# Moving ScalarE's copies out of PSUM behind other work, in a kernel whose order is planned step by step

## The chip, the cores and the metric

One core of one Trainium2 chip runs the whole kernel. Its engines take their instructions in the order in which the program issued them: TensorE (PE; its weight loads are listed as PEld), VectorE (DVE), ScalarE (ACT), GpSimd (POOL) and SyncE (SP, which here only starts transfers). The metric is the device time of one execution in microseconds. Before the change it is 3862.21 us, the median of 13 runs (3836.64 to 3873.43).

## The reference, cut to what matters

Sixteen graphs (B) of 1024 nodes (N) with 64 channels (C); the adjacency matrix is dense in float32, with about 1 in 64 entries nonzero. Four graph layers follow one another, each with a residual and a layernorm:

```python
def reference(x, adj, nodemask, ...):
    # 0: plain graph convolution
    x = _layernorm(x + einsum('bnm,bmo->bno', adj, x @ w0) + b0)
    # 1: thin the neighbours of nodes with more than 10 of them (every skip-th by rank),
    #    then, per node and channel, 0.25/0.5/0.75 quantiles of the neighbours' values
    adj_d = _dilate_adj(adj, nodemask)
    agg = _weighted_nanquantile_agg(x, adj_d > 0)      # sorts, weights 0.25, 0.5, 0.25
    y = relu((x + agg) @ W1 + b1) @ W2 + b2
    x = _layernorm(x + y * nodemask)
    # 2: three layers of messages over the adjacency, 128 wide
    h = x @ W_embed
    for i in range(3):
        h = relu(adj @ (h @ Wl[i] + bl[i]))
    x = _layernorm(x + (h @ W_proj + b_proj) * nodemask)
    # 3: aggregate and compare
    t = adj @ x
    return _layernorm(x + where(t > 0.5, t / t, t * 0.0))
```

## The kernel before, in words

**Tiles.** A graph has T = 8 blocks of 128 nodes (P = 128). A row of 1024 is handled in NH = 2 halves of 512 columns (HALF), which is one PSUM bank of float32; TH = 4 blocks make a half. The tile `adjT` (in the profile `adjB`) holds the transposed adjacency of one graph, 4 MB.

**Strands.** Each graph is worked on by several generators, called strands here:

- `words_of` (line 559): `transposed` (L483) loads the adjacency by blocks of rows, transposes each on PE (L496, two halves of four 128x128 transposes, each half in a bank of the PSUM ring `tp`) and lets ACT copy each half to SBUF (L498, tile `at`; its DMA to DRAM as `adjd` is L590, on ACT's queue). One block later its function `words` compares the block with zero on DVE (L583, L585, tile `nb`), feeds layer 0 (`Layer0.feed`, 8 matmuls at L521 into the single bank `ax`), and packs each row's neighbour bits into words with 8 matmuls (L594, a bank of `tp`), which ACT copies out as `hi` and `lo` (L597, L598). After the fourth and the eighth block ACT copies the bank of layer 0 out (L526). `Layer0.end` (L529) transposes x (L535, ring `tp`), copies it (L537), and finishes the first layer (L542 and a layernorm).
- `front` and `listing` (L613, L647): rank the nodes by their number of neighbours, permute them with one-hot matmuls (L717 on DVE, L722 and L723 on PE), find the neighbours' indices from the words (DVE, L768 to L793), and write a table of node values to DRAM.
- `gathered`, `masked`, `quantiles`, `summed`, for each of five groups of blocks: POOL gathers neighbours' rows from the table (L918); ACT adds a mask to each gathered column of rows (L973); DVE sorts with a network of minima and maxima (L1023); ACT multiplies the sorted rows by weights (L1059) and PE adds them up in the bank `pa` (L1052).
- `back` (L1250): all that follows the quantiles. `to_nodes` (L1083) brings the sums back to the order of the nodes: ACT makes a one-hot matrix for each block from `iota` in two instructions (L1102, L1103, tile `ones_at`, two buffers) and PE multiplies by it (L1107). Then come the two dense layers of layer 1, `to_channels` (L416), three times messages (L1324, copied at L1327) and aggregation (L1335, copied with a ReLU at L1338), the projection, and layer 3 (`aggregate`, L426; L431, copied at L434). Its banks come from the ring `mm`.

The PSUM rings: `mm` 2 banks, `tp` 2, `wd` 2, `ax` 1, and `pa` with part of one. A bank is taken again when the copy out of it is done.

**The order.** Nothing is scheduled by the framework. At the end of the kernel (L1361 to L1431) all strands stand in one queue, sorted by due time. The strand with the smallest due time is run to its next `yield`; what it issues meanwhile goes to the engines' queues in this order, and the yielded number, times the strand's stretch, is added to its due time:

```python
        add(ready - LISTS - WORDS, words_of(state[b]), WORDS / WORDS_STEPS)
        add(start((b + 1) * G) + AFTER, back(state[b]), BACK / BACK_STEPS)
        ...
            dt = next(steps, None)
            if dt is not None:
                heapq.heappush(queue, (t + dt * stretch, order, steps, stretch))
```

So a `yield` is not a wait of the chip: it says how far behind this point, in planned microseconds, the strand's next instruction is put among those of the other strands. A planned graph takes 192.06 us (the sum of LENGTHS, L52). The stretch of `words_of` is 152.6/82, that of `back` 178/181. At a time, the words of one graph, the lists and sorts of others and the back of an earlier one are interleaved.

Of the kernel before, what the change touches and what calls it, by code (L numbers as in the profile page):

```python
# [53 lines left out]
WORDS_STEPS, LISTS_STEPS, BACK_STEPS = 82.0, 74.0, 181.0  # L54
# [152 lines left out]
def kernel(  # L207
# [191 lines left out]
    def psum_tp():  # L399
        return psum("tp", 2)  # L400
# [4 lines left out]
    def psum_ax():  # L405
        return psum("ax", 1)
# [9 lines left out]
    def to_channels(dst, src):  # L416

        for h in range(NH):
# [3 lines left out]
            yield 1.5  # L422
            nc.scalar.copy(dst[:, h * HALF:(h + 1) * HALF], pt[:C, :])
            yield 1.0

    def aggregate(dst, adjT, src, bank):  # L426

        for h in range(NH):
# [5 lines left out]
            nc.scalar.copy(dst[:, h * HALF:(h + 1) * HALF], pa[:C, :])  # L434
            yield 0.7
# [47 lines left out]
    def transposed(b, block, then):  # L483
# [4 lines left out]
        late = None  # L488
        for t in range(T):
            a = ahead[t]  # L490
            at = block(t)
            for h in range(NH):
                pt = psum_tp()
                for i in range(TH):
                    j = h * TH + i
                    nc.tensor.transpose(pt[:, i * P:(i + 1) * P], a[:, j * P:(j + 1) * P], ident)  # L496
                yield 1.2
                nc.scalar.copy(at[:, h * TH:(h + 1) * TH, :],  # L498
                               pt.rearrange("p (i n) -> p i n", n=P))
                yield 0.8  # L500
            if t + AHEAD < T:
                ahead.append(load_row(b, t + AHEAD))
            if late:
                yield from late
            late = then(t, a, at)
        yield 1.0
        yield from late

    class Layer0:
# [6 lines left out]
        def feed(self, t, at):  # L516
            if t % TH == 0:
                self.bank = psum_ax()
# [5 lines left out]
            if t % TH == TH - 1:  # L524
                h = t // TH
                nc.scalar.copy(self.ax[:C, h * HALF:(h + 1) * HALF], self.bank[:C, :])  # L526
                yield 0.7

        def end(self, y):  # L529
            for h in range(NH):  # L530
                pt = psum_tp()
                for i in range(TH):
# [3 lines left out]
                yield 1.0  # L536
                nc.scalar.copy(self.ax[C:, h * HALF:(h + 1) * HALF], pt[C:, :])  # L537
                yield 0.7
# [7 lines left out]
            yield 1.0  # L546
# [12 lines left out]
    def words_of(st):  # L559
# [21 lines left out]
        def words(t, a, at):  # L581
# [4 lines left out]
            if b:  # L586
# [3 lines left out]
                nc.scalar.dma_start(adjd[:, t], at)  # L590
            pw = psum_tp()
# [5 lines left out]
            nc.scalar.copy(hi[:, t, :W], pw[:, :W])  # L597
            nc.scalar.copy(lo[:, t, :], pw[:, W:2 * W + 2])  # L598
            yield 0.6
# [434 lines left out]
    def summed(st, g):  # L1034
# [33 lines left out]
        yield 1.5  # L1068
# [14 lines left out]
    def to_nodes(dst, st):  # L1083
# [12 lines left out]
        for s in range(T):  # L1096
            ones_at = tmp.tile([P, N], BF16, tag="ones_at", name="ones_at", bufs=2)
# [13 lines left out]
        for h, bank in enumerate(banks):  # L1111
# [3 lines left out]
            yield 1.2  # L1115
            nc.scalar.copy(dst[:, h * HALF:(h + 1) * HALF], bank[:C, :])
        yield 1.0
# [131 lines left out]

    def back(st):  # L1250
# [225 lines left out]
```

## Time and profile before

| | us |
|---|---|
| median of 13 runs | 3862.21 |
| the profiled execution | 3866.06 |
| its span, first to last instruction | 3864.3 |
| DVE busy | 2801.8 (73%) |
| PE busy (matmuls) | 2707.7 (70%) |
| POOL busy | 2173.2 (56%) |
| ACT busy | 1902.9 (49%) |
| L1335, aggregation of messages, PE, 1536 records | 818.0, mean 0.653 |
| L973, masks, ACT, 2272 instructions | 597.3, mean 0.339 |
| L498, block of the adjacency out of PSUM, ACT, 240 | 138.0, mean 0.576 |

How it is read: a row of the profile names the line, the engine, the operation, what it writes and reads, how often, the busy time and the mean of one in nanoseconds, and behind the last bar the idle time of the engine just before such instructions with what ended it. "A <- B: 218.2, 31, 20.5" in a list of waits means that A stood idle 218.2 us in all until B ended, 31 times, 20.5 at the longest. "issue" is time in which an engine waited for nothing the profile shows; "remote" is a wait that ended with a signal for which the profile has no instruction ending at that time. The granted clock is the share of TensorE's full clock that was granted: 0.80 on average. The mean TensorE busy time contains time at the lower clock.

### The profile page before, as it was taken

How to read it: one execution, taken by the hardware profiler on the slowest of the kernel's cores; microseconds unless marked ns; L12 is line 12 of the kernel's file. 1: busy time of each engine (PE TensorE's matmuls, PEld its weight loads, DVE VectorE, ACT ScalarE, POOL GpSimd, SP SyncE). 2: the span in 40 equal slices, each digit the busy share in tenths (PEclk: the TensorE clock that was granted, in tenths of full speed). 3: DMA queues.
4: the chain of work that ended last, by engine and by line, in shares of the span. 5: the costliest groups of instructions: out<-in, count | busy, mean ns of one | idle time of the engine just before them, and what ended most of it. 6: DMA issues, size and time to landing. Idle time of an engine off the chain costs nothing.

```text
span 3864.3 us, 49100 instructions
## 1 busy us (share of the span) xinstructions
PE 2707.7 (70%) x13765; PEld 1625.2 (42%) x13766; DVE 2801.8 (73%) x8020; ACT 1902.9 (49%) x6153; POOL 2173.2 (56%) x2078
## 2 busy tenths in 40 slices
PE   6234596867768686686768768677776868675587
PEld 5233353534445353443435444444443535343343
DVE  6287787968687796878769686787867879687561
ACT  2234555545465644545455454636445554545451
POOL 0566655565565655566555665665556556657600
PEclk8656797878878887888878788788887978867788
DMA  3222233232232332223232232323313233212110
GB/s 110 57 78 59 52 83 86 82 93 63 56 98 77 93 82 79 74 61 102 67 92 81 73 85 62 97 73 91 82 36 103 78 87 83 79 23 69 23 50 4
DMA packets 169080, 282.73 MB, mean 73 GB/s; under 512 B 99486, under 2 KB 102113, under 8 KB 166881
## 3 DMA queue, kind: packets, MB, share of 16 engines
q1 hardware_dynamic: 67584, 142.01, 11.1%
q0 software_dynamic: 66048, 69.88, 10.9%
q10 hardware_dynamic: 35168, 67.62, 4.6%
q8 instruction: 114, 1.87, 0.2%
q14 instruction: 166, 1.35, 0.1%
HBM read 204.33 MB, written 71.44 MB: 71 GB/s over the span
## 4 chain that ended last, share of the span: by engine, by line
PE 41%; DVE 19%; another core or an unknown queue 16%; ACT 14%; issue 7%; DMA 1%; POOL 1%; ACTq 0%; DVEq 0%; POOLq 0%
PE mm L1335 15%; PE mm L431 5%; DVE s L1023 5%; DVE g L1023 4%; PE ax L521 4%; ACT g L973 4%; PE mm L1107 3%; PE pa L1052 3%; ACT ones_at L1102 3%; ACT ones_at L1103 2%; PE tp L496 2%; PE mm L1324 2%; ACT g L1059 2%; DVE top L789 1%
## 5 line engine op out<-in xcount | busy, mean ns | idle before, releaser
L918 POOL DMA_INDIRECT g<-table,idx x1952 | 2053.5, 1052 | 1415.5 <-issue 416.9
L1335 PE MATMUL mm<-adjB,msg 128*128 128x512 f32 x1536 | 818.0, 653 | 95.4 <-issue 76.7
L1023 DVE TENSOR_TENSOR s<-g 128x384 f32<-128x384 f32 (+8 forms) x1200 | 577.1, 495 | 281.7 <-ACT g L973 226.6
L973 ACT ACTIVATE g<-g,bias 128x64 f32<-128x64 f32 (+9 forms) x2272 | 597.3, 339 | 82.4 <-DVE bias L969 47.2
L1023 DVE TENSOR_TENSOR g<-s 128x256 f32<-128x256 f32 (+10 forms) x1040 | 508.6, 501 | 27.9 <-remote 14.1
L1052 PE MATMUL pa<-g,ident 128*128 128x128 f32 (+1 forms) x1600 | 342.2, 338 | 208.8 <-ACT g L1059 140.1
L1052 PEld LDWEIGHTS pa<-g,ident 128*128 128x128 f32 x1600 | 284.9, 232 | 358.9 <-ACT g L1059 183.1
L1335 PEld LDWEIGHTS mm<-adjB,msg 128*128 128x128 f32 x1536 | 285.7, 206 | 333.0 <-issue 306.9
L1059 ACT ACTIVATE g<-g,w 128x64 f32<-128x64 f32 x1552 | 392.9, 337 | 13.8 <-DVE w L1030 13.2
L1107 PE MATMUL mm<-ones_at,pieces 128*64 128x512 bf16 x768 | 254.7, 480 | 202.2 <-ACT ones_at L1103 161.3
L521 PE MATMUL ax<-at,xt 128*64 128x128 f32 x1920 | 281.7, 304 | 29.4 <-issue 28.1
L431 PE MATMUL mm<-adjB,x 128*64 128x512 f32 x512 | 274.1, 670 | 11.7 <-DVE x L468 8.9
L521 PEld LDWEIGHTS ax<-at,xt 128*64 128x64 f32 x1920 | 243.3, 154 | 87.6 <-issue 83.0
L496 PE MATMUL tp<-ident,arow 128*128 128x128 f32 x1024 | 176.9, 303 | 86.6 <-ACT lo L598 60.7
L1107 PEld LDWEIGHTS <-pieces 128*64 128x64 bf16 x768 | 97.0, 131 | 315.2 <-issue 272.3
L1023 DVE TENSOR_TENSOR g<-g,s 128x256 f32<-128x256 f32 (+5 forms) x512 | 208.8, 415 | 24.8 <-remote 16.8
L1023 DVE TENSOR_TENSOR g<-g 128x256 f32<-128x256 f32 (+7 forms) x432 | 214.2, 506 | 3.8 <-DVE g L1023 1.5
L1102 ACT ACTIVATE ones_at<-iota,minus 128x1024 bf16<-128x1024 f16 x123 | 140.2, 1140 | 155.1 <-remote 101.1
L496 PEld LDWEIGHTS tp<-ident,arow 128*128 128x128 f32 x1024 | 137.1, 158 | 151.0 <-issue 80.6
L722 PE MATMUL wd<-hi,perm 128*128 128x71 f16 x960 | 107.3, 224 | 132.4 <-DVE perm L717 97.2
L597 ACT CAST hi<-tp 128x64 f16<-128x64 f32 x128 | 26.6, 208 | 352.0 <-remote 204.0
L1338 ACT ACTIVATE hlT<-mm 128x512 f32<-128x512 f32 x96 | 57.2, 596 | 267.6 <-PE mm L1335 190.5
(223 smaller groups left out, 4262.8 us busy)
## 6 DMA issues: line engine op xcount, KB each, us to landing
arow<-in_adj_dram SPq DMA_DIRECT2D x128, 512.0 KB
adjd<-at ACTq DMA_DIRECT2D x120, 512.0 KB
adjB<-adjd SPq DMA_DIRECT2D x15, 4096.0 KB
g<-table,idx POOLq DMA_INDIRECT x1952
table<-xc ACTq DMA_DIRECT2D x16, 264.0 KB
xt<-in_x_dram SPq DMA_DIRECT2D x16, 256.0 KB
out_dram<-y SPq DMA_DIRECT2D x16, 256.0 KB
stage<-table,packed POOLq DMA_INDIRECT x112
```

The costliest lines, as they stand in the source:

```text
L431: nc.tensor.matmul(pa[:C, :], src[:, m, :], adjT[:, h * TH:(h + 1) * TH, m, :], start=(m == 0), stop=(m == T - 1))
L496: nc.tensor.transpose(pt[:, i * P:(i + 1) * P], a[:, j * P:(j + 1) * P], ident)
L521: nc.tensor.matmul(self.bank[:C, cols], self.xt[:, m + 1, :], at[:, m, :], start=(m == 0), stop=(m == T - 1))
L722: nc.tensor.matmul(pw[:, :hn], ws, hi[:, t, :], start=False, stop=False)
L918: g = nc.gpsimd.indirect_dma_start(out=dst, out_offset=None, in_=st["table"], in_offset=bass.IndirectOffsetOnAxis(ap=index, axis=0))
L973: nc.scalar.activation(v, v, AF.Identity, bias=bias[:m, i, k:k + 1])
L1023: vector.tensor_tensor(box(bufs[mode >> 1 & 1], d, run, sd, count, tile), box(bufs[mode >> 3], a, run, sa, count, tile), box(bufs[mode >> ...
L1052: nc.tensor.matmul(pa[:, :(e - k) * nt * C], ident, rows_.rearrange("p (k c) -> p k c", c=R)[:, :, :C], start=(j == 0), stop=(j == len(run ...
L1059: nc.scalar.activation(slots(g, bufs[0], lo + r, lo + r + 1)[:, i, 0, :C], slots(g, bufs[at[r]], lo + r, lo + r + 1)[:, i, 0, :C], AF.Iden ...
L1102: nc.scalar.activation(ones_at, iota, AF.Abs, bias=st["minus"][:, s:s + 1])
L1107: nc.tensor.matmul(bank[:C, :], pieces[:, i, s, :], ones_at[:, h * HALF:(h + 1) * HALF], start=(s == 0 and i == 0), stop=False)
L1335: nc.tensor.matmul(pg, msg[:, m, :], adjT[:, h * TH:(h + 1) * TH, m, :], start=(m == 0), stop=(m == T - 1))
```

## The change

No instruction is added and none is removed; the steps are put in another order, by moving `yield`s and the calls between them.

- Adjacency (`transposed`): both halves of a block are transposed first. The copy of the first half is issued after the feed of the block before (at a `yield None` in `words`), the copy of the second half after that block's words matmuls.
- Words: `hi` and `lo` are copied not at once, but as a function `write` that is kept and called after the first half of the next block's transposes.
- Layer 0: the copy of the first half's bank goes just ahead of the fifth block's feed; that of the second half, and those of x, behind all transposes of `end`.
- Back: in `to_channels`, `to_nodes` and the dense layers (new function `hidden`) both halves are multiplied first, then both copied. In the message layers the copies of a half fall behind matmuls of the other half; the last half of a layer's ReLU (`late`) falls behind the first half of the next layer's messages.
- Some waits of DVE on PE's results (`residual`, the layernorm of layer 0, layer 3) get more steps ahead of them.
- `ones_at` has three buffers in place of two.
- WORDS_STEPS and BACK_STEPS, by which the stretches are formed, are 83 and 203.

```diff
-WORDS_STEPS, LISTS_STEPS, BACK_STEPS = 82.0, 74.0, 181.0
+WORDS_STEPS, LISTS_STEPS, BACK_STEPS = 83.0, 74.0, 203.0
     def to_channels(dst, src):
+        banks = []
         for h in range(NH):
             pt = psum_mm()
             for i in range(TH):
                 nc.tensor.transpose(pt[:C, i * P:(i + 1) * P], src[:, h * TH + i, :], ident)
-            yield 1.5
+            banks.append(pt)
+            yield 1.0
+        yield 2.5
+        for h, pt in enumerate(banks):
             nc.scalar.copy(dst[:, h * HALF:(h + 1) * HALF], pt[:C, :])
-            yield 1.0
+            yield 0.8
     def aggregate(dst, adjT, src, bank):
...
                 yield 1.3
-            nc.scalar.copy(dst[:, h * HALF:(h + 1) * HALF], pa[:C, :])
-            yield 0.7
+                if h and m == TH - 1:
+                    nc.scalar.copy(dst[:, :HALF], banks[0][:C, :])
+            banks.append(pa)
+        yield 3.0
+        nc.scalar.copy(dst[:, HALF:], banks[1][:C, :])
+        yield 0.7
     def transposed(b, block, then):
...
-        late = None
+        late, written = None, []
         for t in range(T):
+            banks = []
...
             for h in range(NH):
-                pt = psum_tp()
+                banks.append(psum_tp())
...
-                yield 1.2
-                nc.scalar.copy(at[:, h * TH:(h + 1) * TH, :],
-                               pt.rearrange("p (i n) -> p i n", n=P))
-                yield 0.8
+                yield 0.9
+                if h == 0 and written:
+                    written.pop()()
+                    yield 0.6
             if t + AHEAD < T:
                 ahead.append(load_row(b, t + AHEAD))
-            if late:
-                yield from late
+            def moved(h, at=at, banks=banks):
+                nc.scalar.copy(at[:, h * TH:(h + 1) * TH, :],
+                               banks[h].rearrange("p (i n) -> p i n", n=P))
+            first = True
+            for dt in late or [2.0]:
+                if callable(dt):
+                    written.append(dt)
+                elif dt is None:
+                    moved(0)
+                    first = False
+                    yield 0.7
+                else:
+                    yield dt
+            if first:
+                moved(0)
+                yield 0.7
+            moved(1)
+            yield 0.7
             late = then(t, a, at)
...
         def feed(self, t, at):
             if t % TH == 0:
+                if t:
+                    self.copied(t // TH - 1)
+                    yield 0.5
                 self.bank = psum_ax()
...
         def end(self, y):
...
-                yield 1.0
+                yield 0.7
+            yield 2.0
+            self.copied(NH - 1)
+            yield 0.6
+            for h, pt in enumerate(banks):
                 nc.scalar.copy(self.ax[C:, h * HALF:(h + 1) * HALF], pt[C:, :])
-                yield 0.7
+                yield 0.6
...
         def words(t, a, at):
...
                 nc.scalar.dma_start(adjd[:, t], at)
+            yield None
             pw = psum_tp()
...
-            nc.scalar.copy(hi[:, t, :W], pw[:, :W])
-            nc.scalar.copy(lo[:, t, :], pw[:, W:2 * W + 2])
-            yield 0.6
+            def write():
+                nc.scalar.copy(hi[:, t, :W], pw[:, :W])
+                nc.scalar.copy(lo[:, t, :], pw[:, W:2 * W + 2])
+            yield write
...
-            ones_at = tmp.tile([P, N], BF16, tag="ones_at", name="ones_at", bufs=2)
+            ones_at = tmp.tile([P, N], BF16, tag="ones_at", name="ones_at", bufs=3)
...
+    def hidden(w_sb, src, hT, copy):
+        banks = [psum_mm() for _ in range(NH)]
+        for h, ph in enumerate(banks):
+            nc.tensor.matmul(ph, w_sb, src[:, h * HALF:(h + 1) * HALF], start=True, stop=True)
+            yield 1.3
+        yield 2.0
+        for h, ph in enumerate(banks):
+            copy(hT[:, h * HALF:(h + 1) * HALF], ph)
+            yield 0.7
     def residual(src, w_sb, first, base, y):
...
-            yield 1.0
+            yield 3.5
             u = wide_u("u")
...
         for l in range(NL):
+            def give(h):
+                nc.scalar.copy(msg[:, h * TH:(h + 1) * TH, :],
+                               parts.pop(("msg", h)).rearrange("p (i k) -> p i k", k=H))
             for h in range(NH):
+                if h:
+                    if late:
+                        late()
+                        yield 0.7
                 pg = psum_mm()
...
+                parts["msg", h] = pg
+            give(0)
+            yield 1.0
+            new = act.tile([H, N], F32, tag="hT", name="hlT")
             for h in range(NH):
                 pg = psum_mm()
                 for m in range(T):
+                    if h == 0 and m == TH:
+                        give(1)
+                        yield 1.0
                     nc.tensor.matmul(pg, msg[:, m, :], adjT[:, h * TH:(h + 1) * TH, m, :],
                                      start=(m == 0), stop=(m == T - 1))
                     yield 1.3
-                nc.scalar.activation(hT[:, cols], pg, AF.Relu)
-                yield 0.7
+                    if h and m == TH - 1:
+                        nc.scalar.activation(new[:, :HALF], parts.pop("first"), AF.Relu)
+                parts["second" if h else "first"] = pg
+            def late(new=new):
+                nc.scalar.activation(new[:, HALF:], parts.pop("second"), AF.Relu)
...
-        yield 2.0
+        yield 4.0
         u = wide_u("u3")
```

## The prediction

> **What bounds the kernel now.** I read the page first, for busy shares and the chain that ended last:
>
> ```profile
> span 3864.3 us, 49100 instructions
> PE 2707.7 (70%) x13765; PEld 1625.2 (42%) x13766; DVE 2801.8 (73%) x8020; ACT 1902.9 (49%) x6153; POOL 2173.2 (56%) x2078
> PE 41%; DVE 19%; another core or an unknown queue 16%; ACT 14%; issue 7%; DMA 1%; POOL 1%; ACTq 0%; DVEq 0%; POOLq 0%
> ```
>
> No engine is full, and the chain passes from one engine to the next: the bound is waiting in fixed orders. Next came the table by stretches (columns: length, then PE, weight loads, DVE, ACT, POOL busy, granted clock, DMA share, GB/s). The first row is the steady part, where one graph takes about 228 us (the same weight-summing step recurs at 1414.7, 1643.0 and 1870.6 us in the chain); the other two lie 19 us apart inside one graph.
>
> ```profile
> 400.00:3400.00 3000.00, 2207.43 (x11360) 1309.08 (x11361) 2287.65 (x6491) 1578.04 (x5072) 1795.19 (x1705) 0.82 0.29 79
> 1434.00:1453.00 19.00, 14.68 (x85) 9.16 (x83) 18.67 (x44) 7.98 (x28) 14.09 (x13) 1.00 0.22 51
> 1453.00:1472.00 19.00, 6.45 (x16) 3.84 (x17) 4.17 (x14) 4.22 (x17) 11.04 (x11) 0.60 0.14 25
> ```
>
> DVE is busy 2288 of 3000 us, so 712 us are idle, about 54 per graph; and there are moments, like the last row, when PE, DVE and ACT all stand. Whom they wait for, over the same 3000 us (total, times, longest):
>
> ```profile
> DVE s L1023 <- ACT g L973: 218.2, 31, 20.5
> DVE u L1275 <- PE mm L1269: 47.9, 14, 11.2
> DVE perm L717 <- remote: 41.5, 9, 8.3
> DVE perm L717 <- PE mm L1107: 25.2, 6, 6.8
> DVE u L1350 <- PE mm L1347: 24.0, 11, 3.0
> PE mm L1107 <- ACT ones_at L1103: 138.5, 47, 11.5
> PE ax L542 <- ACT ax L537: 17.1, 4, 7.3
> PE mm L1335 <- ACT msg L1327: 14.7, 6, 13.2
> ```
>
> The largest wait of DVE is for the masks (L973) that ACT puts on gathered rows. Why is ACT late, at 49%? The groups by line say where it sits idle (after the second bar):
>
> ```profile
> L1102 ACT ACTIVATE ones_at<-iota,minus 128x1024 bf16<-128x1024 f16 x123 | 140.2, 1140 | 155.1 <-remote 101.1 <-PE wd L723 21.4 <-PE mm L1107 20.1
> L1338 ACT ACTIVATE hlT<-mm 128x512 f32<-128x512 f32 x96 | 57.2, 596 | 267.6 <-PE mm L1335 190.5 <-remote 58.8 <-issue 15.7
> L1327 ACT COPY msg<-mm 128x512 f32<-128x512 f32 x96 | 55.9, 582 | 204.6 <-remote 150.4 <-issue 26.5 <-PE mm L1324 26.4
> L597 ACT CAST hi<-tp 128x64 f16<-128x64 f32 x128 | 26.6, 208 | 352.0 <-remote 204.0 <-PE tp L594 123.4 <-PE pa L1052 9.4
> L537 ACT COPY ax<-tp 64x512 f32<-64x512 f32 x32 | 18.4, 581 | 153.5 <-remote 135.7 <-issue 13.0 <-PE tp L535 4.7
> ```
>
> These four copies and ones_at alone hold 1133 of ACT's 1961 us of idle time (3864.3 − 1902.9). The timeline of the standstill shows what that does:
>
> ```profile
> 1457.13 0.21 ACT L597 CAST hi<-tp 128x64 f16<-128x64 f32 x1 [14.01 <-remote]
> 1458.00 1.74 PE L1052 MATMUL pa<-g,ident 128*128 128x128 f32 x6 [9.31 <-ACT g L1059]
> 1470.01 0.60 ACT L1338 ACTIVATE hlT<-mm 128x512 f32<-128x512 f32 x1 [10.64 <-remote]
> 1471.13 0.80 PE L1052 MATMUL pa<-g,ident 128*128 128x128 f32 x2 [7.56 <-ACT g L1059]
> 1476.85 0.42 DVE L1023 TENSOR_TENSOR s<-g 128x256 f32<-128x256 f32 x1 [19.58 <-ACT g L973]
> ```
>
> ACT stands 14.0 and 10.6 us before two copies out of PSUM; behind them in its queue are the weightings (L1059) for which PE stands, and the masks for which DVE stands 19.6 us. "Remote" means that nothing the profile shows ended then: PE's signal came later than the modelled end of its matmul. I don't know why. What matters is that ACT meets it at the head of its queue.
>
> **The change, part by part.** The profiled execution took 3866.06 us (span 3864.3 and 1.8 around it), 3.85 above the median of 3862.21; I sum against 3866. The change adds no instruction and no byte: the same copies of 0.57 to 0.67 us (0.21 for hi and lo) are issued later in the planned order, so every cost is a wait.
>
> *Adjacency and words.* A block's steps run at 152.6/82 = 1.86 us of planned time before, 152.6/83 = 1.84 after. Transposes to copy: 1.2 steps (2.2 us) before; after, the first copy comes behind 0.9 + 0.6 + 0.9 + 0.3 + 2.4 = 5.1 steps (9.4 us). Words matmul to hi: 0.7 steps (1.3 us) before; 0.7 + 0.7 + 0.9 = 2.3 (4.2 us) after. What ACT loses there now (352 us at L597, 100 at L498) mostly goes.
>
> *Layer 0* (L526, L537), *back* (L1338, L1327, L434, L423, L1116): each copy falls behind 2 to 3.5 steps or behind four further matmuls of the same line. The back has more steps, but its step shrinks from 178/181 = 0.98 to 178/203 = 0.88 us, so its planned length hardly changes and its matmuls are issued a tenth denser.
>
> *Gain at the masks.* Between nothing and the 218 us of that wait. In the standstill shown, ACT lost 24.6 us at two moved copies for DVE's 19.6, so the nearest row says all; but some of what ACT is late with waits for DVE itself (the bias of the masks), and PE's late signal stays in the world. I take 60%: 130 us.
>
> *Gain from the third one-hot buffer.* With two, ACT must wait for the matmuls of two one-hots ago, PE for ACT, and DVE's permutations (L717) for PE: 41.5 + 25.2 and 14.6 more behind another matmul of PE, 81 us. ACT needs 1.14 + 1.06 us for each one-hot whatever the buffers, so between nothing and 81; I take half, 40.
>
> *Gain at u* (L1275, L1350): these waits of DVE, 47.9 + 24.0, get 3.5 and 4.0 steps in place of 1.0 and 2.0. Half: 36. In the last 214 us, the last back alone, DVE's long waits for PE are the work itself; I count nothing there.
>
> *Price: PSUM is held longer.* All rings keep their sizes (mm 2, tp 2, ax 1). So the tight side changes over: before, a bank was emptied 4 to 5.5 steps ahead of its next use; now PE's words matmul stands 0.7 steps (1.3 us) behind the copy that frees its bank, the next transposes 0.7, the second transposes 0.6, and the fifth block's feed 0.5 behind the copy of layer 0. PE takes work in order, so a late ACT now stops everything behind: feeds, L1335, the sums pa. Some 25 such links a graph in the words and 10 in the back make 490 in 14 graphs. Nearest rows: PE's waits at links that are already so short, 14.7 us over 96 message copies (0.15 each) and 17.1 over 32 copies of ax (0.53 each): 75 to 260 us of PE. Below nothing is possible only if the copies come earlier, which none does; zero is possible if ACT runs ahead. PE makes 41% of the chain: 0 to 107 us of the time. I take 0.3 a link: 147 × 0.41 = 60.
>
> The granted clock bears on that price: 1.00 while PE is busy, 0.60 in the standstill, and a pair of L1335 takes 1.02 us at 1447.7 and 1.92 at 1461.7. [...]
>
> *Queues moved past.* SP's row loads are issued between the same transposes and wait for them as before; ACT's adjacency writes wait for copies made a block earlier; the gathers on POOL follow DVE, whose order changes little. DVE's comparison of a block (L583) now stands 3.1 steps behind its last copy instead of 8: 5.7 us, ten times the copy. If ACT is later than that, DVE's sorts queue behind it.
>
> **Sum.** −130 − 40 − 36 + 60 = −146: 3866 − 146 = 3720 us.
>
> **The rivals.** *The tight links decide (slower, 0.22).* PE waits for ACT at 490 places. For it: PE is in the chain more than ACT, and already waits 138.5 us for ones_at. Against it: copies with short links now cost PE little, because ACT, with 1422 idle us in 3000, is mostly ahead. If only a third of my gains comes (69 us) and links cost 0.7 us, 343 × 0.41 = 141: 3866 − 69 + 141 = 3938. It decides from 0.34 us a link on (69/0.41/490).
>
> *Nothing is gained where it counts (0.10).* ACT's idle time is a symptom of PE's late signals; the copy waits as long in its new place, or DVE waits for the next thing, PE's sums. Then gain and price are both small: 3866 within 0.3%, 3854 to 3878. For it: 16% of the chain is time that the profile gives to no engine, and an order of copies does not touch its cause. Against it: three engines stand while the needed work lies behind one copy.
>
> *All of it goes (0.08).* −200 − 60 − 50 + 20: 3576. Then DVE would be busy 2288 of 2710 us, 84%, against 76 now; nothing forbids it, but each removed wait uncovers another.
>
> **How the numbers follow.** My forecast has 0.60, and by itself 3620 to 3845. The measurement can tell about 0.3%. Faster by more: 0.59 + 0.08 + 0.03 of the second rival = 0.70; within: 0.07 of the second rival and 0.01 of the forecast, 0.08; slower: 0.22. For 8 in 10 the range takes part of the fastest case and the nearer part of the slower one: 3580 to 3905.
>
> **What would show it.** Right: ACT's idle time at hi, hlT, msg and ax falls from 978 us to less than half; DVE's wait for the masks falls from 227 to about 90, and 19 us standstills become rare; PE shows new waits for the copies at, hi/lo and ax at transposes and words, in all 75 to 260 us. Wrong: DVE's wait for the masks stays though ACT's idle moved; or PE's waits at tp and ax exceed 300 us; or the clock falls below 0.80.

## The result: 2.0% slower, and the profile after

The changed kernel took 3937.3 us (median of 10 runs, 3928.8 to 3943.1), the kernel before 3860.5 (46 runs): ratio 1.0201, interval 1.0182 to 1.0219. I had forecast 3720.

One thing is needed to read what follows. Within one set of runs a kernel repeats to some tenths of a percent, but between sets the kernel before took 3867.4 us (e1 to e4), 3154.0 (e5 to e8), 3780.2 (e9 to e12), 3157.5 (e13 to e16) and 3151.8 (e17, e18). So every ratio below is to the kernel before in the same set. The sets above 3700 us, like the run on record, show stretches in which PE crawls (called phases below); those near 3155 show none. The last section tells of them. The change loses in both kinds: 1.0201 above, and 1.032 (1.0303 to 1.0337) in e13.

The page of the changed kernel:

```profile
span 3930.8 us, 49137 instructions
PE 2752.4 (70%) x13765; PEld 1660.7 (42%) x13766; DVE 2800.3 (71%) x8020; ACT 1902.2 (48%) x6153; POOL 2181.5 (55%) x2078
PE 35%; DVE 25%; another core or an unknown queue 13%; ACT 10%; issue 9%; DMA 2%; POOL 1%; DVEq 0%; ACTq 0%; POOLq 0%; SPq 0%
```

Busy time is as before; what grew is waiting, and DVE has taken part of PE's place in the chain. DVE's waits over the same 3000 us as before (total, times, longest):

```profile
DVE u L1337 <- PE mm L1331: 226.0, 14, 19.8
DVE cand L817 <- ACT wd L808: 120.3, 11, 16.7
DVE perm L766 <- remote: 76.4, 10, 13.9
DVE nb L628 <- ACT at L516: 70.6, 32, 5.1
```

The 218.2 us at the masks are gone from the list (10.5 are left in the whole span). In their place stand 226.0 us at `u` (47.9 before), once a graph and as long as the old ones. PE's waits:

```profile
PE mm L1398 <- ACT msg L1372: 84.5, 11, 11.7
PE wd L764 <- DVE below L754: 68.0, 13, 6.6
PE mm L1156 <- ACT ones_at L1152: 63.7, 20, 4.8
```

The third buffer did what it should (138.5 to 63.7); the messages' copy costs PE 84.5 where it cost 14.7. The groups that were to lose ACT's idle time (after the second bar):

```profile
L645 ACT CAST hi<-tp 128x64 f16<-128x64 f32 x128 | 26.6, 208 | 370.7 <-remote 316.8 <-PE tp L640 45.3 <-issue 5.7
L1372 ACT COPY msg<-mm 128x512 f32<-128x512 f32 x96 | 55.7, 581 | 205.2 <-remote 162.5 <-PE mm L1384 39.5 <-issue 3.2
L1402 ACT ACTIVATE hlT<-mm 128x512 f32<-128x512 f32 x48 | 28.7, 598 | 124.3 <-PE mm L1398 104.0 <-remote 20.4
L1407 ACT ACTIVATE hlT<-mm 128x512 f32<-128x512 f32 x48 | 28.8, 599 | 85.3 <-PE mm L1398 75.1 <-PE pa L1101 6.2 <-remote 4.0
L582 ACT COPY ax<-tp 64x512 f32<-64x512 f32 x32 | 18.5, 582 | 13.7 <-issue 13.0 <-PE tp L576 0.3
```

Together 799 us, 978 before; the sum was to fall below half. And the timeline of one standstill, all engines:

```profile
1486.71 0.27 PE L1101 MATMUL pa<-g,ident 128*128 128x128 f32 x1 [1.18 <-issue]
1490.26 0.80 PE L561 MATMUL ax<-at,xt 128*64 128x128 f32 x3 [1.69 <-issue]
1493.81 0.37 PE L561 MATMUL ax<-at,xt 128*64 128x128 f32 x1 [0.74 <-issue]
1495.25 0.21 ACT L645 CAST hi<-tp 128x64 f16<-128x64 f32 x1 [17.52 <-remote]
1504.06 0.69 DVE L1337 TENSOR_TENSOR u<-mm,mb 128x512 f32<-128x512 f32 x1 [18.37 <-PE mm L1331]
```

It is a standstill of the same kind as the one in the prediction, near the same point of the graph: the `u` that follows it starts at 1484.33 us before and at 1504.06 here. PE itself goes on only now and then ("issue": it waits for nothing that is shown), ACT stands at `hi` as before, and DVE now stands at `u` instead of at a sort that needs masks.

How much DVE waits in all is read from the table by stretches, over exactly ten graphs (third to thirteenth output transfer; columns as before, DVE is the third busy time). Before, then after:

```profile
1081.40:3351.40 2270.00, 1684.92 (x8600) 995.75 (x8600) 1734.97 (x4931) 1190.09 (x3850) 1361.83 (x1291) 0.82 0.29 80
```

```profile
1082.10:3399.60 2317.50, 1709.99 (x8600) 1026.57 (x8600) 1734.22 (x4932) 1191.90 (x3851) 1368.99 (x1291) 0.79 0.29 78
```

DVE's work is the same (1735.0, 1734.2); its idle time is 535.0 and 583.3. The 47.5 us by which ten graphs are longer are DVE's idle time (48.3 more), and with 18.3 us more behind the thirteenth output (531.2 against 512.9) and 0.7 ahead of the third they make the 66.5 of the two spans. So the question for the experiments: why does DVE wait more, when its largest wait was taken away?

### The profile page after: what moved, and what is told of

Read it like the earlier page. It is cut to its first block, busy times and chain, and to the rows that moved or that the text cites. A ratio compares the mean times of both kernels' runs of the same rounds, so it can differ in the third digit from the quotient of the medians.

```text
span 3930.8 us, 49137 instructions
## 1 busy us (share of the span) xinstructions
PE 2752.4 (70%) x13765; PEld 1660.7 (42%) x13766; DVE 2800.3 (71%) x8020; ACT 1902.2 (48%) x6153; POOL 2181.5 (55%) x2078
## 4 chain that ended last, share of the span: by engine, by line
PE 35%; DVE 25%; another core or an unknown queue 13%; ACT 10%; issue 9%; DMA 2%; POOL 1%; DVEq 0%; ACTq 0%; POOLq 0%; SPq 0%
PE mm L1398 16%; DVE g L1072 7%; DVE s L1072 6%; PE ax L561 4%; ACT g L1022 4%; PE pa L1101 3%; PE mm L436 2%; PE mm L1384 2%; ACT ones_at L1151 2%; PE tp L506 2%; PE mm L1156 2%; PE mm L1331 1%; ACT ones_at L1152 1%; DMA g<-table,idx 1%
## 5 line engine op out<-in xcount | busy, mean ns | idle before, releaser
L1398 PE MATMUL mm<-adjB,msg 128*128 128x512 f32 x1536 | 778.4, 628 | 118.5 <-ACT msg L1372 93.2
L1072 DVE TENSOR_TENSOR s<-g 128x384 f32<-128x384 f32 (+8 forms) x1200 | 574.1, 495 | 24.1 <-ACT g L1022 10.5
L1398 PEld LDWEIGHTS mm<-adjB,msg 128*128 128x128 f32 x1536 | 274.7, 200 | 327.8 <-issue 222.8
L561 PE MATMUL ax<-at,xt 128*64 128x128 f32 x1920 | 296.7, 305 | 82.9 <-issue 81.9
L1337 DVE TENSOR_TENSOR u<-mm,mb 128x512 f32<-128x512 f32 x32 | 22.1, 690 | 352.6 <-PE mm L1331 298.9
L506 PE MATMUL tp<-ident,arow 128*128 128x128 f32 x1024 | 190.6, 321 | 96.5 <-ACT lo L646 52.8
L506 PEld LDWEIGHTS tp<-ident,arow 128*128 128x128 f32 x1024 | 145.1, 166 | 203.0 <-issue 123.9
L628 DVE TENSOR_SCALAR nb<-at 128x1024 f16<-128x1024 f32 x120 | 84.2, 701 | 176.2 <-ACT at L516 124.9
```

The lines of the kernel that those rows point to most:

```text
L506: nc.tensor.transpose(banks[h][:, i * P:(i + 1) * P], a[:, j * P:(j + 1) * P], ident)
L561: nc.tensor.matmul(self.bank[:C, cols], self.xt[:, m + 1, :], at[:, m, :], start=(m == 0), stop=(m == T - 1))
L628: vector.tensor_scalar(nb, at, 0.0, None, op0=ALU.is_gt)
L1072: vector.tensor_tensor(box(bufs[mode >> 1 & 1], d, run, sd, count, tile), box(bufs[mode >> 3], a, run, sa, count, tile), box(bufs[mode >> ...
L1398: nc.tensor.matmul(pg, msg[:, m, :], adjT[:, h * TH:(h + 1) * TH, m, :], start=(m == 0), stop=(m == T - 1))
```

## The experiments

**First set: the parts alone.** Four edits of the kernel before.

e1: adjacency, words and layer 0 of the change (and WORDS_STEPS 83), nothing else.

> Adjacency, words and layer 0 as in the changed kernel; back, the sums' yield and the one-hot buffers as before. Theory 'tight links' (the loss of 77 us is PE waiting at banks that ACT empties later): new PE waits stand at both places, about three quarters of the links are here, so 40 to 60 us of the loss come here. Theory 'late PE' (copies are not where the time goes; the standstill is PE's own and the plan only decides who is seen waiting for it): DVE's wait for the masks falls here already, and DVE's waits for PE grow by as much; time within 1% of before (3822 to 3899).

Measured 3909.4 us, ratio 1.0123 (1.0082 to 1.0164). In ten graphs the wait for the masks is 91.8 (184.8 before), and 101.5 us stand at `nb` <- `at`, where the kernel before has none in its list: the comparison that now follows 3.1 steps behind its copy.

e2: the back of the change alone (with BACK_STEPS 203, two one-hot buffers, and 3.0 steps in place of 1.5 ahead of the copy of the sums, an edit of the change that the list above leaves out).

> Back alone (channels, nodes, dense layers, messages, aggregation, the longer yields ahead of u and u3, 203 steps, and the longer yield ahead of the sums' copy); adjacency, words, layer 0 and two one-hot buffers as before. 'Tight links': the wait of PE for msg (84.5 us after, 14.7 before) and for tT (39.0, 4.7) is here, about 110 us of PE, 41% of it on the path: 45 us slower than before. 'Late PE': the waits of DVE for u (226 us after, 47.9 before) are back here only if the back's own order makes PE late; time 3900 to 3940, with slow phases of PE as often as in the changed kernel.

Measured 4058.7 us, 1.0484 (1.0432 to 1.0536): more than the whole change. PE's waits for `msg` and `tT` are not what did it (24.3 us for `msg`); DVE's wait for `u` is 231.9 in ten graphs (36.8 before). Neither theory had the size.

e3: three buffers.

```diff
-            ones_at = tmp.tile([P, N], BF16, tag="ones_at", name="ones_at", bufs=2)
+            ones_at = tmp.tile([P, N], BF16, tag="ones_at", name="ones_at", bufs=3)
```

> Three one-hot buffers alone. My prediction's term: 40 us faster (3820), PE's wait for ones_at falls from 138.5 us to under 70 as in the changed kernel. 'Late PE': PE runs ahead at the one-hots and stands elsewhere; 0 to 10 us.

Measured 3849.4 us, 0.9953 (0.9926 to 0.9980): PE's wait for `ones_at` fell to 34.7 in 3000 us, and 18 us of the 3867 came of it. This one line is faster than the kernel before in that set.

e4: does PE's crawl depend on where its code lies?

```diff
     vector.tensor_copy(mask, pm[:, :B * T])
+    for _ in range(64):
+        nc.tensor.matmul(pm[:16, 400:401], ones16[:, :16], ones16[:, :1], start=True, stop=True)
```

> The kernel before with 64 tiny matmuls (one column, 128 instructions of PE with their weight loads) put in at the start, after the mask's transposition; their result is not used. They take about 4 to 8 us where PE waits for loads anyway. [...]

Measured 3872.6, 1.0023 (1.0000 to 1.0046). The phases stay at about the same steps: three of them begin at 1382.5, 1612.4 and 1833.6 us before, and at 1372.3, 1604.8 and 1828.1 here, where the third output comes 13 us earlier. A shift of PE's code by 128 instructions (64 matmuls, each with its weight load) does not move them. The 4 to 8 us for the matmuls were an estimate of mine; no row here shows their own time, and the whole is 5 us longer (3867.4 to 3872.6).

**Second set: without gathers, without stage transfers.**

```diff
-            g = nc.gpsimd.indirect_dma_start(
-                out=dst, out_offset=None, in_=st["table"],
-                in_offset=bass.IndirectOffsetOnAxis(ap=index, axis=0))
+            g = nc.gpsimd.memset(dst, 1.0)
```

> The kernel before with every gather of table rows (POOL, indirect DMA) replaced by a memset of the same rows on POOL; the neighbours' values are left out, all else stays, the eight stage transfers of SP too. Theory 'late signals under gathers' (the phases in which PE goes on at one instruction per 0.7 us and its signals come 10 to 25 us late arise only while POOL gives out gathers without a pause): the phases vanish, 278 us of them before to under 50, and the time falls by at least 5%, under 3680. If the phases are PE's own: 200 us or more of them stay, and the time falls by less than 2%.

> The changed kernel with the same replacement (gathers left out). 'Late signals under gathers': the loss of 2% goes with the phases; this is no slower than the kernel before without gathers, or up to 2% faster, since the copies then wait less. 'Tight links' (PE waits for ACT at banks that are emptied later): it stays 1.5 to 3% slower than the kernel before without gathers.

Measured 3087.0 us (0.9788, 0.9771 to 0.9805) and 3196.3 (1.0136, 1.0119 to 1.0153). But in this set the kernel before took 3154.0 us and no run shows a phase, so nothing follows on what starts them. What does follow: the changed kernel without gathers is 3.5% slower than the kernel before without gathers (3196.3 / 3087.0). The loss needs neither gathers nor late signals. POOL's 2050 us of gathers are worth 2% here.

```diff
-                    src = st["stage", q // 2][first:first + m, q % 2:q % 2 + len(ks)]
-                    nc.sync.dma_start(dst, src)
+                    pass
-                        vector.memset(slots(g, buf, full, n)[:, i2], BIG)
+                        vector.memset(slots(g, buf, full, n)[:, i2], 1.0)
```

> The kernel before without SP's transfers g<-stage (eight a graph, of a few rows each); the slots they fill keep a constant, which is left out of the result's meaning; gathers stay. If these short transfers on SP start the slow phases (most phases begin 4 to 9 us after them): phases fall to about half, 140 us, time 1 to 3% less, 3750 to 3825. If gathers alone make them: as before within 0.5%.

> The changed kernel without the same transfers g<-stage. If they start the phases: 398 us of them fall to under 200 and the time comes within 0.5% of the kernel before without them. If not: 2% slower than that, about 3935.

Measured 3157.1 us (1.0009, 1.0000 to 1.0019) and 3261.8 (1.0347, 1.0330 to 1.0364). The transfers cost nothing here, so e7's profile can stand for the kernel before in a set without phases, and e13, the changed kernel itself, for the one after. There the picture is clean. Ten graphs of e7, and DVE's waits in them:

```profile
872.80:2692.20 1819.40, 1521.05 (x8600) 934.09 (x8600) 1728.50 (x4931) 1181.77 (x3850) 1385.15 (x1288) 0.91 0.35 99
```

```profile
DVE u L1274 <- PE mm L1268: 15.8, 10, 3.3
DVE u L1349 <- PE mm L1346: 15.0, 10, 1.5
DVE cand L768 <- ACT wd L759: 14.2, 10, 1.8
DVE ln_v L454 <- ACT sq L451: 9.6, 10, 1.6
```

Ten graphs of e13:

```profile
894.30:2791.20 1896.90, 1550.21 (x8600) 954.80 (x8600) 1729.76 (x4931) 1191.86 (x3851) 1387.96 (x1292) 0.88 0.34 96
```

```profile
DVE u L1337 <- PE mm L1331: 41.4, 10, 4.2
DVE ln_v L463 <- ACT sq L460: 39.6, 10, 4.8
DVE cand L817 <- ACT wd L808: 29.6, 10, 3.0
DVE u L1423 <- PE mm L1420: 19.2, 10, 1.9
DVE nb L628 <- ACT at L516: 3.3, 10, 0.4
```

DVE is the bound here, busy 95% of the ten graphs of e7, and of the 77.5 us more 76.2 are its idle time again: 90.9 to 167.1. It waits once a graph and always at the same places, longest at the `u` of the last residual. The two `u` take 29.8 us of the 76.2 (30.8 to 60.6), the layernorm of layer 0 (`ln_v`) 30.0, `cand` 15.4. In the timeline of e13, PE stands nowhere in the 14 us ahead of the `u` of the last residual; it is simply late:

```profile
1417.02 1.96 PE L561 MATMUL ax<-at,xt 128*64 128x128 f32 x16
1419.64 2.00 PE L1331 MATMUL mm<-wp_sb,hlT 128*128 128x64 f32 x16
1421.68 0.69 DVE L1337 TENSOR_TENSOR u<-mm,mb 128x512 f32<-128x512 f32 x1 [4.14 <-PE mm L1331]
1425.20 0.59 ACT L1108 ACTIVATE g<-g,w 128x64 f32<-128x64 f32 x2 [1.00 <-DVE w L1079]
1425.84 0.80 PE L1101 MATMUL pa<-g,ident 128*128 128x128 f32 x2 [3.94 <-ACT g L1108]
```

The last two lines show what the wait costs further on: behind `u` in DVE's queue are the sorts and the sum `w`; ACT needs `w` to weight rows, and PE then stands 3.94 us for the weighted rows. PE is late again for what comes next; that DVE's waits at `ln_v` and u3 follow from this is my reading, no run shows it.

PE's lateness at this `u` is not a matter of the clock here. In the 14 us that end with the projection's last matmul (L1331, L1268 or L1269) PE is busy 13.99 us or more at a granted clock of 1.00, in each of the ten graphs of e7, e13, e14 and e17. PE is full there in all four; the plan decides how much other work DVE has left to do meanwhile: DVE is busy 9.6 to 9.7 us of the 14 in e13, 10.2 to 12.9 in e7.

**Third set: which part, with phases again.**

e9 is the change with its back as before, e10 the change with adjacency, words and layer 0 as before; both have three buffers.

> The changed kernel with its back undone: adjacency, words, layer 0 and three one-hot buffers, the back as before. All in ratios to the kernel before in the same runs, since that took 3867 us in the first four runs and 3154 us in the next four. Theory 'the back's order' (the copies and yields of the back make PE late for u, and DVE waits): 1.00 or less, with DVE's wait for u as before. Theory 'words and layer 0': 1.015 or more, with DVE's wait ln_v<-sq and nb<-at grown.

> The changed kernel with adjacency, words and layer 0 undone: the back and three one-hot buffers. 'The back's order': 1.02 to 1.04, the wait of DVE for u doubled as in the changed kernel. 'Words and layer 0': 1.01 or less.

Measured 1.0252 (1.0187 to 1.0316) and 1.0544 (1.0478 to 1.0610). Each half alone loses; in e9 DVE waits 138.4 us in ten graphs at `nb` <- `at`, in e10 207.9 at `u`.

e11: the changed kernel with `Layer0` as before (its `feed`, `end` and 1.0 step ahead of its layernorm).

```diff
-            yield 3.0
+            yield 1.0
             yield from layernorm(nodes(pz), y, "0")
```

> The changed kernel with Layer0 alone as before (feed and end: its copies at once, and 1.0 step ahead of its layernorm). In the runs without slow phases the changed kernel's DVE waits 45.8 us for sq in 2300 us against 12.7 before, because the last matmuls of layer 0 then stand among the dense matmuls of the back's aggregation. If that place is a cause: the wait falls to about 13 and the time by 1 to 1.4% against the changed kernel (ratio about 1.022 where that has 1.034, 1.01 where it has 1.020). If it is only where lateness of PE shows: the wait goes to u or cand and the time stays within 0.4% of the changed kernel.

Measured 1.0410 (1.0346 to 1.0474). A miss: DVE's wait for `sq` is 85.6 in ten graphs and did not fall (30.0 in the changed kernel on record). Layer 0's place is not where the loss comes from; it looks rather like a gain, since with layer 0 as before DVE waits almost three times as long there (the two profiles are of different sets).

e12: `u` later.

```diff
-            yield 3.5
+            yield 6.5
             u = wide_u("u")
```

> The changed kernel with 6.5 steps in place of 3.5 ahead of u in the residuals (2.6 us of plan later; no other edit). 'DVE waits at u because u is put too early': the wait for u goes (49 us in 2300 without slow phases), and the time falls by 1% or more. 'PE is late and the wait moves on': DVE waits less for u and as much more elsewhere, time within 0.5% of the changed kernel or above it.

Measured 1.0154 (1.0098 to 1.0211). The wait at `u`, 168.2 us in ten graphs of the changed kernel on record, is down to 4.4; 157.8 stand at the masks again and 113.1 at `nb`. The wait moved on, as the second theory said, but this is the smallest ratio of the set. How it compares with the changed kernel is not settled, since that was not in this set (1.0201 on record).

**What the plan says about `u`.** That sent me back to the arithmetic of the plan, which I had not done. The due time of `u` in the last residual, after the planned start of the back, is its wait for the sums and the sum of the yields up to it times the length of a step. Before: 67.5 us to the first message, then three message layers of 29.8 steps, 89.4 x 0.983 = 87.9 us, then 5 steps of residual, 4.9: 160.3 us. After: 71.3 us to the first message (the added yields, those ahead of the copy of the sums among them, for which the back waits), then the same layers with 89.3 steps, now of 0.877 us, 78.3 us; then 7.5 steps, 6.6: 156.2 us. With 3.5 steps in front of it in place of 1.0, `u` is due 4.1 us EARLIER, because a step was shortened to keep the planned length and the message layers, which got no steps, gave up 9.6 us.

**Fourth set: the step against the copies** (no phases).

e13 is the changed kernel, its numbers are above.

> The changed kernel itself, so that the others of this set can be compared with it in the same runs. 1.02 where the kernel before shows slow phases, 1.03 where it shows none.

Measured 1.0320 (1.0303 to 1.0337).

```diff
-WORDS_STEPS, LISTS_STEPS, BACK_STEPS = 82.0, 74.0, 181.0
+WORDS_STEPS, LISTS_STEPS, BACK_STEPS = 82.0, 74.0, 203.0
```

> The kernel before with BACK_STEPS 203 alone: no copy moved, no yield added; the back ends 19 us sooner in the plan and u of x3 is due 17 us sooner (142.9 us after the back's start, 160.3 before, 156.2 in the changed kernel). 'The step is the cause': DVE's waits for u at least double and the kernel is slower than before by 2% or more. 'The place of the copies is the cause': the ratio is within 0.99 to 1.01.

Measured 1.0575 (1.0556 to 1.0594). The shorter step without any moved copy costs almost twice what the change does. DVE's waits in ten graphs:

```profile
DVE u L1275 <- PE mm L1269: 80.2, 10, 8.8
DVE u L1350 <- PE mm L1347: 65.3, 10, 7.0
DVE cand L768 <- ACT wd L759: 42.0, 10, 4.3
```

The waits at the two `u`, 30.8 us in e7, are 145.5. That a back put earlier makes DVE wait at `u`, and costs time, is shown. Whether it is the place of `u` by itself or that of all PE's work in the back is not, since the step moves both. (This run moves `u` 16.5 us, to 143.8 when the order's queue is stepped through with its yields; the change moves it 4.1.)

e15: the changed kernel with BACK_STEPS 190 in place of 203.

> The changed kernel with BACK_STEPS 190: every copy where the change puts it, the step 0.937 us in place of 0.877 (0.983 before), u of x3 due 166.9 us after the back's start. 'The step is the cause': the wait for u goes and the time falls by 1.5% or more against the changed kernel, to 1.005 or less. 'The place of the copies': within 0.5% of the changed kernel.

Measured 1.0395 (1.0376 to 1.0413): a miss. The wait at `u` went as expected, but others came:

```profile
DVE ag L1126 <- ACT half L1125: 54.4, 16, 8.1
DVE nb L628 <- ACT at L516: 16.6, 8, 3.3
DVE cand L817 <- ACT wd L808: 13.8, 12, 2.8
```

e16: no copy moved, three buffers, `u` and u3 later.

```diff
-            yield 1.0
+            yield 3.0
             u = wide_u("u")
-        yield 2.0
+        yield 4.0
         u = wide_u("u3")
```

> The kernel before with three one-hot buffers and 3.0 and 4.0 steps ahead of u and u3 in place of 1.0 and 2.0, the step's length as before (0.983 us; u of x3 due 4 us later than before). If putting u later is what pays: 0.985 to 0.995. If the wait only moves on: that of the three buffers alone, about 0.995 to 1.0.

Measured 1.0419 (1.0394 to 1.0445), the same way: 70.2 us at `ag`, and PE stands up to 16.5 us at a one-hot.

These two runs do not test what their expectations say, a `u` that is 6.6 or 4 us later. Their backs no longer fit into a graph. Stepping through the order's queue with each kernel's yields, a back takes 196.1 us (e15) and 195.1 us (e16) of plan from its start in `to_nodes` to its end, where a planned graph has 192.06; before it is 189.2, in the changed kernel 183.5. A back does not begin before the one ahead of it is done, so each graph's back is put 3 to 6 us further behind the rest of the plan: `u` of x3 is due 165.9 us after the planned start in the first graph and 230.1 in the sixteenth (e15), 163.7 and 215.4 (e16). In the plan a sum is copied out only after the back ahead has read its own, so the sums fall behind too, and that is where DVE waits (`ag`). What these runs show is the price of a back that is longer than a graph; what a `u` a few us later than before costs in a back that fits, no run without phases tried.

**Fifth set: `u` where it was, copies moved** (no phases).

e17: the changed kernel with BACK_STEPS 197.8, so that `u` of the last residual is due 178.1 steps x 0.900 = 160.3 us after the start, as before. (Here the back fits: 188.3 us of plan.)

> The changed kernel with BACK_STEPS 197.8 alone: the step is 0.900 us, u of x3 is due 160.3 us after the back's start as before the change (156.2 in the changed kernel), u3 1.4 us later than before. 'The due place of u is the cause': DVE's wait for u falls back to the level of before and half of the loss or more goes: 1.016 or less without slow phases, 1.01 or less with them. 'The moved copies are the cause': the loss stays within 0.5% of the changed kernel (1.032 without slow phases, 1.020 with them).

Measured 1.0188 (1.0173 to 1.0202): 1.3 points better than e13. The wait at `u` is gone from DVE's list, as the first theory expected, but the ratio stays above its 1.016.

e18: the same step with adjacency, words and layer 0 as before.

> The same step of 0.900 us, back and three one-hot buffers changed, adjacency, words and layer 0 as before the change. If the words and layer 0 carry the rest of the loss: 1.00 to 1.01. If the back's copies carry it: within 0.5% of e17.

Measured 1.0109 (1.0094 to 1.0125).

The waits of DVE in ten graphs of e17:

```profile
DVE nb L628 <- ACT at L516: 41.0, 10, 5.0
DVE cand L817 <- ACT wd L808: 29.3, 10, 3.1
DVE ln_v L463 <- ACT sq L460: 14.2, 10, 1.4
```

and of e18:

```profile
DVE ln_v L463 <- ACT sq L460: 33.5, 20, 3.0
DVE cand L777 <- ACT wd L768: 30.3, 10, 3.1
DVE u L1297 <- PE mm L1291: 12.2, 10, 1.3
```

The sets without phases in one table (ten graphs, us; idle is length less busy):

| kernel | step | `u` of x3 due | ten graphs | DVE busy | DVE idle | ratio |
|---|---|---|---|---|---|---|
| e7, before (without stage) | 0.983 | 160.3 | 1819.4 | 1728.5 | 90.9 | 1.0009 |
| e14, step alone | 0.877 | 143.8 | 1962.3 | 1733.0 | 229.3 | 1.0575 |
| e13, the change | 0.877 | 156.2 | 1896.9 | 1729.8 | 167.1 | 1.0320 |
| e17, the change, `u` as before | 0.900 | 160.3 | 1860.6 | 1731.3 | 129.3 | 1.0188 |
| e18, and words as before | 0.900 | 160.3 | 1853.0 | 1728.6 | 124.4 | 1.0109 |
| e16, `u` later, no copy moved | 0.983 | 164 to 215 | 1940.7 | 1755.2 | 185.5 | 1.0419 |
| e15, the change, longer step | 0.937 | 166 to 230 | 1928.9 | 1762.0 | 166.9 | 1.0395 |

(In e15 and e16 the stretch holds 80 and 62 more DVE instructions, so a little more work: the outputs fall behind the rest.) Of the 3.2% that the change costs here, 1.3 points go when the step is 0.900 us and `u` is due where it was; 0.8 more when adjacency, words and layer 0 are as before. Of these 25 us (3208.8 to 3183.9 of span) 7.6 lie in the ten graphs and 13.3 ahead of them; `nb` <- `at`, 41.0 us in e17, is gone in e18, and most of it comes back in the other waits. 1.1 points stay with the back, its buffers and the sums' later copy, in waits at `ln_v` and `cand` that I did not take apart.

## Why the prediction was wrong, step by step

**The gain at the masks (130 us).** The step that failed first. The wait did go, from 227 us to 10.5 in the span, more than I had said; the time did not. I priced a wait of DVE by its own length. What counts is DVE's idle time as a whole, and that rose from 535.0 to 583.3 in ten graphs: behind the removed wait stood the next, at `u`, for a late PE. The second rival said this of the gain ("DVE waits for the next thing"), and I gave it 0.10 because three engines stood behind one copy. ACT stood there because PE was late (ACT stands 17.5 us at `hi` in the changed kernel too), and moving the copy did not make PE earlier.

**The gain at u (36 us).** Wrong in sign: 47.9 us became 226.0, where I had taken half away. I counted the steps ahead of `u` (1.0 to 3.5) and noted that the step shrinks and that the matmuls come a tenth denser, but did not follow the due time through: 4.1 us earlier, with PE asked to do the message layers in 78.3 us in place of 87.9. This is the part of the loss for which there are experiments, without phases: the shorter step alone costs 5.75% (e14), and a step that puts `u` back where it was takes 1.3 of 3.2 points away (e17). Both move the whole back; no run without phases moves `u` alone, and on record, with phases, none tries the step alone.

**The third buffer (40 us).** PE's wait fell as I had said, from 138.5 to 63.7 (34.7 in e3), and e3 is 18 us faster (8 to 29). But the row from which I priced it did not move: DVE's waits at `perm`, of which I took half, are 67.2 us in ten graphs before and 67.3 in e3. The term is more than twice too large, and where its 18 us came from is open.

**The tight links (price 60 us).** PE's waits for the moved copies (`lo`, `at`, `ax`, `msg`, `oT`, `hT`, `hlT`, `tT`), in ten graphs: 32 us before and 105 after on record, nearly all in `msg` (61) and `tT` (34) and hardly any at the transposes and words, where I had put most links; 14 in e7 and 20 in e13. On record that is about 100 us more in 14 graphs, by my share of 0.41 some 42 us of time (an estimate), so the price was not far off. But the loss does not need it: without phases the growth is 6 us and the loss is larger, and e2 loses 4.8% with 24.3 us at `msg` and 3.7 at `tT`. The rival that held the right sign, 3938 us beside a measured 3937.3, met the number by luck: no run shows its price of 141 us, and its gains of 69 us were not there.

**DVE's comparison behind its last copy.** I named it (5.7 us of plan, "ten times the copy") and priced it at nothing. It is a cost: 70.6 us of waits at `nb` on record, 101.5 and 138.4 with the words alone, 41.0 in e17. (Before, the comparison stood 8.8 steps behind its copy, by the yields, not 8.)

**The clock.** My sum has no term for it. The granted clock fell in the ten graphs, from 0.82 to 0.79 on record and from 0.91 (e7) to 0.88 (e13) without phases. Without phases it is not what makes DVE wait at `u`, as the clock of 1.00 ahead of it shows. L1398 takes 610 ns (e13) where the same line took 611 (e7); other lines got longer (L1305 on `x2T` 1012 against 727), and PE's busy time in ten graphs grew by 29 us, so it is not shown that the clock has no part in the rest of the loss. On record the clock is low just there: in the 14 us that end with the projection, it is 0.50 in nine of the ten graphs of the changed kernel, PE is busy 9.1 to 9.9 of them and DVE not at all, where the kernel before has 0.50 to 0.92. In the standstill shown above PE's pauses are "issue" (1.18, 1.69 and 0.74 us ahead of the three rows) and not waits for a bank. How much of the 2% is the crawl and how much the clock, no run separates.

**What was to show it.** The mask wait near 90 and less than half of ACT's idle time: 10.5 and 799 of 978. The signs said "wrong" at the clock below 0.80 (0.777), and the sign for "right" at ACT's idle time did not come. A shorter wait at the masks was a poor sign: it came, and the kernel got slower.

Open: why the whole change (1.0201) loses less than its back with three buffers (1.0544) when there are phases; those are two sets of runs with different times before (3860.5 and 3780.2), and the pair was not run in one set. A pointer is the layernorm of layer 0: the two kernels with layer 0 as before, e10 and e11 (1.0410), wait 94.8 and 85.6 us at `ln_v` in ten graphs, the whole change 30.0.

## What to carry to other kernels

In a hand-planned order, work out where the plan now puts each instruction, in microseconds from the strand's start, before you count added steps: if the length of the strand is kept, every yield added in one place takes time from all others. Size the gain of a removed wait by the idle time of the bounding engine as a whole, and ask which late producer the wait stood for; when the producer stays late, the wait reappears at its next consumer (here 227 us at the masks became 10.5, and 47.9 at `u` became 226.0). Check too that a strand still fits into its period: e15 and e16 lose 4% with backs of 196 and 195 planned us in a graph of 192. And test the constant that scales a plan by itself (e14: one number edited, 5.75%).

## What the runs showed of the hardware

PE crawls. I count stretches in which successive instructions of PE (matmuls and weight loads) start together or 0.705 us or a multiple apart, to within 0.05 us, with at least six such steps. The profile before has 21 of them, 192 us in all, the changed kernel 16 with 142, e12 28 with 283, so their sum does not go with the time; the profiles of e5 to e8 and of e13 to e18 have none. (The 278 and 398 us in the expectations of e5 and e8 are of another count; that the changed kernel has more of them does not come out of this one.) Here one matmul of the words after another, L594 of the kernel before, where eight of them otherwise take 0.42 us:

```profile
1386.01 0.21 PE L594 MATMUL tp<-pow,nb 128*128 128x65 f16 x1 [1.23 <-issue]
1388.12 0.21 PE L594 MATMUL tp<-pow,nb 128*128 128x65 f16 x1 [1.90 <-issue]
1388.85 0.21 PE L594 MATMUL tp<-pow,nb 128*128 128x65 f16 x1 [0.52 <-issue]
1389.56 0.23 PE L594 MATMUL tp<-pow,nb 128*128 128x65 f16 x1 [0.50 <-issue]
```

In this stretch the matmuls themselves take 0.19 to 0.23 us each, where the median of all 1024 of the line is 0.194; and in such stretches signals come late, by some 21 us in e2: ACT stood 24.98 us ahead of `hi` until 1287.05, where the profile has the last matmul of that bank end at 1266.01. This is the "remote" of the prediction. Most of the stretches come once a graph near the same steps, and moving PE's code by 128 instructions left them there. In three sets of runs they are absent, in all kernels, and then the same kernel takes 3152 to 3157 us in place of 3780 to 3867, the share "another core or an unknown queue" (16% before, on record) is gone from the chain, and DVE is busy 95% of the ten graphs (e7). What makes them come and go stays open. It is not in the kernel, and the chip with number 3 in the record shows both kinds (e1 to e4 with, e5 to e8 without), as does number 4 (e9 to e12, e17 and e18). Since no run without gathers fell into a set that has them, whether they need the gathers was not settled either.
